# A decoder layer with routed experts on one core: expert results scattered to the tokens' rows, two routing phases run as one pipeline after the attention, and two heads per column group of the values product

## The chip, the cores and the metric

The kernel runs on one core of a Trainium2 chip. The metric is device microseconds of one execution; the median of three runs is given. A core has TensorE for matrix products (PE; its weight loads, PEld, overlap them), VectorE (DVE), ScalarE (ACT), GpSimd (POOL) and SyncE (SP), which here only issues transfers. Each engine works through its own instructions in order, and they meet through semaphores. Sixteen DMA engines move data for all of them.

## The reference

32 sequences of 128 tokens, width 128. All is float32.

```
x = layernorm(x + attention(x, x, x, causal))          # 16 heads of 8
x = layernorm(x + attention(x, ctx, ctx))              # cross attention
r = softmax(x @ router_w + router_b)                   # 8 experts
topw, topi = top_k(r, 2); topw = softmax(topw)
h_e = gelu(x @ w1[e] + b1[e])                          # 128 -> 512, exact gelu
o_e = h_e @ w2[e] + b2[e]                              # 512 -> 128
x = layernorm(x + sum over the token's two experts of topw * o_e)
```

The reference computes all experts for all tokens and weighs six of eight by zero. The kernel computes most tokens for their two experts only.

## The kernel before

**Attention.** A group is four sequences; there are eight groups of self attention ("s") and eight of cross attention ("c"). A unit is one sequence of one kind, 64 in all. `order` (L873) puts eleven self units first, then one cross and one self in turn, then the last eleven cross units. Time in the program is counted in half slots, two to a unit: `half_slot(h)` (L947) issues the scores of the newest unit and the transposed scores of the one two before it (`both_scores`, L355), each half of 16 heads; the maximum over keys (DVE, L390), the exponential (ACT, L398), and for self attention the causal mask (POOL, L402). In even half slots follow the values product of the unit three back (`values`, L429) and the turning of the newest maxima; in odd ones the splitting of maxima (POOL, L407) and `outputs` (L443), which transposes the result, divides by the sum and stores it. The values of a group lie in one of three tiles `vs` (L213), nine columns a head: eight values and a one, which makes the sum. A values product takes 32 such columns as its weights, so its result has 32 rows a head, of which nine are used; four heads stand above one another and four such sets fill a bank.

After that, `half_slot` runs whatever `table` holds for h: fetching inputs, transposing them, projections of keys, queries and values, `project` (output projection, residual and norm), `keep_x2`, `route` (top two experts and their weights, five steps), `place` (five steps) and `scatter`. Thus the order on every engine is written out by hand: `at(h, call)` fixes it.

**Routing.** Groups 0 to 3 are phase 0, groups 4 to 6 phase 1. `place` gives each of a token's two choices a row in `xs`, a DRAM buffer cut in blocks of 128 rows that belong to one expert each: eight first blocks, one an expert, and up to 31 or 23 more, whose expert stands in `ph.tab`. `scatter` (L634) sends tokens' rows there by indirect DMA on POOL, two of 128 rows in a half slot. `clear` has zeroed the rows that nobody fills.

**Blocks** (L675). For each block SP fetches its expert's packed weights (578 KB, `wd`, five buffers, four ahead); for four blocks at once it fetches rows (`xt`), PE transposes them and DVE copies them out (`turn`). `first_layer` is four products and four GELUs on ACT; `second_layer` of the block before is four products into one tile, to which DVE adds the bias (L755) into `ot`; after four blocks SP stores `ot` to `eo` in the same order of rows. Phase 0's 39 blocks run at half slot 117, between two stretches of attention (`BURST`); phase 1's 31 run after the last scatter.

**Sums.** `gather` (L780) brings a token's two result rows from `eo` by indirect DMA on POOL; `combine` (L791) adds them to the token's row by weight, on DVE, and `finish` norms and stores it. Phase 0's gathers lie in the half slots after the first blocks, phase 1's beside the dense group.

**Dense group** (L817). Group 7 isn't scattered. All eight experts are computed for its 512 tokens at the end, with a product of 512 columns, and each result is added by its weight, which is zero for most.

Constants and parameters are set up ahead of everything (L130 to L267), on all queues; nineteen parameter loads are issued from ACT's queue and the others from SP's. The main order, L966 on:

```
for h in range(-2, 2 * BURST + 3): half_slot(h)
bursts[0].run(lambda: None)
...          # half slots until the last scatter
bursts[1].prepare()
bursts[1].run(beside)
...          # dense group, with the gathers and sums of phase 1 beside it
```

Of the kernel before, what the change touches and what calls it, by code (L numbers as in the profile page):

```python
# [17 lines left out]
P = 128  # L18
# [6 lines left out]
PHASES = ((0, 4), (4, 3))  # L25
NP = len(PHASES)
LAST = 7
# [12 lines left out]
VS = HD + 1  # L40
NPART = 3
LEAD = 11
BURST = 57
# [15 lines left out]
def kernel(  # L59
# [69 lines left out]
    groups = {(kind, gi): Group(kind, gi) for kind in "sc" for gi in range(NG)}  # L129
    fetch(groups["s", 0])  # L130

    def load(src, shape, name, queue=nc.scalar):
        t = const.tile(shape, F32, name=name)
        queue.dma_start(out=t, in_=src)
        return t

    def column(src, name, queue=nc.scalar):
        return load(src.rearrange("(p o) -> p o", o=1), [P, 1], name, queue)
# [6 lines left out]
    class Attn:  # L145
        def __init__(self, wq, bq, wk, bk, wv, bv, wo, n):
            self.wk = load(wk, [P, P], f"wk{n}")
            self.bk = column(bk, f"bk{n}")
            self.wq = load(wq, [P, P], f"wq{n}")
            self.bq = column(bq, f"bq{n}")  # L150
            self.wv = load(wv, [P, P], f"wv{n}")
            self.wo = load(wo, [P, P], f"wo{n}")
            self.bv = column(bv, f"bv{n}")

    sa = Attn(sa_wq, sa_bq, sa_wk, sa_bk, sa_wv, sa_bv, sa_wo, "s")
# [4 lines left out]

    causal = const.tile([P, RG, P], BF16, name="causal")
    nc.gpsimd.memset(causal, 0.0)
    nc.gpsimd.affine_select(
        out=causal,
        in_=causal,
        pattern=[[0, RG], [-1, P]],
        compare_op=ALU.is_ge,
        fill=MASKED,
        base=0,
        channel_multiplier=1,  # L170
    )
# [22 lines left out]

    mp4 = setup.tile([P, RG, NPART, 4], F32, name="mp4")
# [9 lines left out]
    ones16 = const.tile([P, P], BF16, name="ones16")  # L205
    nc.gpsimd.memset(ones16, 1.0)
# [4 lines left out]


    vs = [const.tile([P, G, H * VS + VC - VS], F32, name=f"v_{i}") for i in range(3)]  # L213
    for t in vs:
        nc.gpsimd.memset(t, 0.0)
        nc.gpsimd.memset(
            t[:, :, : H * VS].rearrange("p b (h c) -> p b h c", c=VS)[:, :, :, HD:], 1.0
        )
    apart = const.tile([1, 1], F32, name="apart")
    mhalf = const.tile([P, G], F32, name="mhalf")  # L220
    nc.gpsimd.memset(mhalf, -0.5)

    def counted(shape, pattern, base, name, pool=const):
# [7 lines left out]
    bo_s = row(sa_bo, P, "bo_s")  # L231
    ca = Attn(ca_wq, ca_bq, ca_wk, ca_bk, ca_wv, ca_bv, ca_wo, "c")
    head_bias(ca, "c")
    bo_c = row(ca_bo, P, "bo_c")
    lng = [row(a, P, f"lng{i}") for i, a in enumerate((ln1_g, ln2_g, ln3_g))]
    lnb = [row(a, P, f"lnb{i}") for i, a in enumerate((ln1_b, ln2_b, ln3_b))]
    lngT = [column(a, f"lngT{i}") for i, a in enumerate((ln1_g, ln2_g))]
    lnbT = [column(a, f"lnbT{i}") for i, a in enumerate((ln1_b, ln2_b))]
    rw = load(router_w, [P, E], "rw")
    rb = row(router_b, E, "rb")  # L240
    b1 = setup.tile([E * NFC, P], F32, name="b1")
    nc.sync.dma_start(out=b1, in_=e_b1.rearrange("e (c f) -> (e c) f", f=P))


    iota_e = counted([P, E], [[1, E]], 0, "iota_e")
    before16 = const.tile([P, P], BF16, name="before16")
    nc.gpsimd.affine_select(
        out=before16, in_=ones16, pattern=[[1, P]], compare_op=ALU.is_gt,
        fill=0.0, base=0, channel_multiplier=-1,
    )  # L250
    full = counted([P, E, G], [[0, E], [P, G]], 0, "full")
    e_col = counted([P, E, E], [[1, E], [0, E]], 0, "e_col", setup)
    e_row = counted([P, E, E], [[0, E], [1, E]], 0, "e_row", setup)
    lower = const.tile([P, E, E], F32, name="lower")
    nc.vector.tensor_tensor(lower, e_row, e_col, ALU.is_lt)
    d_at = counted([P, max(ND), E], [[1, max(ND)], [0, E]], NS, "d_at")
    zero = const.tile([P, P], F32, name="zero")
    nc.gpsimd.memset(zero, 0.0)
# [5 lines left out]
    xs = [tc.dram_tile([NBL[p] * P, P], F32, name=f"xs_{p}") for p in range(NP)]  # L264
    eo = [tc.dram_tile([NBL[p] * P, P], F32, name=f"eo_{p}") for p in range(NP)]
# [69 lines left out]
    turn = {"v": 0, "m": 0}  # L335
# [93 lines left out]
    def values(u):  # L429
        po = mm_tile([P, RG, P], f"po_{u.name}")  # L430
        for g in range(RG):
            for r in range(4):
                h = 4 * g + r
                nc.tensor.matmul(  # L434
                    po[VC * r : VC * r + VC, g, :],
                    lhsT=u.group.v[:, u.b, VS * h : VS * h + VC],
                    rhs=u.pr[:, h, :], start=True, stop=True,
                )
        u.group.done += 1
        u.uT = prob.tile([P, RG, P], F32, tag="uT", name=f"uT_{u.name}")  # L440
        nc.scalar.copy(u.uT, po)

    def outputs(u):  # L443
        if u.b == 0:
            u.group.o = act.tile([P, G, P], F32, tag="o", name=f"o_{u.group.name}", bufs=3)
        pu = mm_tile([P, RG, 4, VC], f"pu_{u.name}")
        for g in range(RG):
            nc.tensor.transpose(pu[:, g].rearrange("p r c -> p (r c)"), u.uT[:, g, :], ident)
        pu = pu.rearrange("p g r c -> p (g r) c")
        ri = small.tile([P, H], F32, tag="ri", name=f"ri_{u.name}")  # L450
        nc.vector.reciprocal(ri, pu[:, :, HD])
        nc.vector.tensor_tensor(
            u.group.o[:, u.b, :].rearrange("p (h d) -> p h d", d=HD),
            pu[:, :, 0:HD],
            bc(ri, 2, HD),
# [32 lines left out]
    def keep_x2(gr):  # L488
        gr.x2T = affineT(gr, 1)
        gr.x2 = act.tile([P, G, P], F32, tag="x2", name=f"x2_{gr.gi}", bufs=3)  # L490
        nc.gpsimd.tensor_tensor(gr.x2, gr.y, bc(lng[1], 1, G), ALU.mult)
        nc.gpsimd.tensor_tensor(gr.x2, gr.x2, bc(lnb[1], 1, G), ALU.add)
        if gr.gi != LAST:
            nc.sync.dma_start(
                out=x2d[G * gr.gi : G * gr.gi + G].rearrange("b p d -> p b d"), in_=gr.x2
            )

    def route(gr):
# [31 lines left out]
        nc.vector.tensor_copy(idf, idx[:, :, 0:2])  # L530
        gr.onehot = small.tile([P, 2, G, E], F32, tag="onehot", name=f"onehot_{gi}", bufs=2)
        for k in range(2):
            nc.vector.tensor_tensor(
                gr.onehot[:, k], bc(iota_e, 1, G), bc(idf[:, :, k], 2, E), ALU.is_equal
# [9 lines left out]
    class Phase:  # L544
# [6 lines left out]
        def __init__(self, p):  # L551
            self.p, self.sent, self.first = p, [], True
# [3 lines left out]
    def place(gr, ph):  # L556
# [7 lines left out]
        if ph.first:  # L564
# [8 lines left out]
            nc.gpsimd.tensor_scalar(ph.at, iota_e, float(P), float(P), ALU.mult, ALU.add)  # L573
# [8 lines left out]
        nc.vector.tensor_tensor(over, bc(tot, 2, G), full, ALU.is_gt)  # L582
# [42 lines left out]
        nc.vector.tensor_tensor(which, bc(end, 1, ND[p]), d_at[:, : ND[p], :], ALU.is_le)  # L625
# [3 lines left out]
        if gi == PHASES[p][0] + PHASES[p][1] - 1:  # L629
            ph.tab = slot.tile([P, ND[p]], I32, tag=f"tab{p}", name=f"tab{p}")  # L630
            nc.vector.tensor_copy(ph.tab, ph.sums)
            nc.vector.tensor_scalar(ph.tab, ph.tab, E - 1, None, ALU.bitwise_and)

# [35 lines left out]
    def clear(p):  # L669
        nc.sync.dma_start(out=xs[p].rearrange("(n p) d -> p n d", p=P), in_=bc(zero, 1, NBL[p]))  # L670
# [4 lines left out]
    class Blocks:  # L675
# [3 lines left out]
        def __init__(self, ph):  # L679
            self.ph, self.n = ph, NBL[ph.p]  # L680
            self.xt, self.xT, self.ot, self.w, self.h = {}, {}, {}, {}, {}
# [7 lines left out]
        def fetch_rows(self, q):  # L689
# [3 lines left out]
            self.xt[q] = moe.tile([P, XB, P], F32, tag="xt", name=f"xt_{p}_{q}", bufs=1)  # L693
# [21 lines left out]
        def turn(self, q):  # L715
# [5 lines left out]
            for j in range(n):  # L721
                nc.tensor.transpose(px[:, j, :], xt[:, j, :], ident)
# [331 lines left out]
```

## Time and profile before

| | us |
|---|---|
| median of 3 runs (798.76 to 801.45) | 801.38 |
| the profiled execution | 799.84 |
| its span, first to last instruction | 798.1 |
| PE busy | 626.9 (79%) |
| PE weight loads busy | 505.7 (63%) |
| DVE busy | 419.4 (53%) |
| ACT busy | 370.7 (46%) |
| POOL busy | 326.4 (41%) |
| DMA moved | 84.46 MB, 106 GB/s over the span |

A profile page gives busy time, the same in 40 slices of the span, the DMA queues, the chain of work that ended last, and the costliest groups of instructions by line, each with its busy time, the mean of one in ns, and the idle time of its engine just before it with what ended that. Times of the prediction are of the one profiled execution, so its sum is made against 799.84.

### The profile page before, as it was taken

The page shows a single profiled execution, that of the slowest core. Times are in us where ns is not written, and L with a number is a line of the kernel's source. Part 1 is how long each engine was busy: PE and PEld are TensorE (multiplying, and loading weights), DVE is VectorE, ACT ScalarE, POOL GpSimd, SP SyncE. Part 2 cuts the span into 40 slices and gives each one's busy share as a digit, 9 for nine tenths or more (in the row PEclk, how much of TensorE's full clock was granted, in tenths as well). Part 3 has the DMA queues.
Part 4 walks back from the last instruction along what each step waited for, and adds up shares of the span by engine and source line. Part 5 has one row for each costly group of instructions (what it writes and reads, how often), then busy time and mean ns, then how long its engine had stood idle before and what let it go on. Part 6 is the DMA issues. An engine that isn't in the chain of part 4 may idle for free.

```text
span 798.1 us, 21600 instructions
## 1 busy us (share of the span) xinstructions
PE 626.9 (79%) x8943; PEld 505.7 (63%) x8995; DVE 419.4 (53%) x1242; ACT 370.7 (46%) x668; POOL 326.4 (41%) x616
## 2 busy tenths in 40 slices
PE   1889888889889889889988999985821299968882
PEld 0466667677667667667767899974721199835552
DVE  1344665657866767857867222275777222102574
ACT  0256565665655555645556655642300155523220
POOL 3135654425475474483572000058787300052320
PEclk9799999999999999999999999997855599979996
DMA  3060605301001001001023899712131689862121
GB/s 80 1 147 3 146 16 161 86 3 43 2 25 44 2 29 42 3 28 29 19 76 122 277 359 347 269 32 84 51 96 34 211 275 347 310 217 68 45 77 28
DMA packets 74115, 84.46 MB, mean 106 GB/s; under 512 B 7680, under 2 KB 61216, under 8 KB 74016
## 3 DMA queue, kind: packets, MB, share of 16 engines
q1 hardware_dynamic: 67696, 75.18, 29.6%
q0 software_dynamic: 3584, 7.35, 3.1%
q8 instruction: 71, 1.16, 0.6%
q10 hardware_dynamic: 2736, 0.53, 0.3%
q14 instruction: 28, 0.23, 0.1%
HBM read 66.25 MB, written 21.51 MB: 110 GB/s over the span
## 4 chain that ended last, share of the span: by engine, by line
PE 49%; POOL 16%; DVE 11%; DMA 11%; ACT 7%; issue 5%; SPq 1%; ACTq 0%; POOLq 0%; DVEq 0%
DMA wd<-wpk 8%; POOL xs L640 6%; PE st_s L375 5%; PE ph L733 5%; PE phd L848 4%; PE po L751 4%; PE pod L861 4%; PE po_s L434 3%; POOL gt L786 3%; PE st_c L375 2%; DVE m_s L390 2%; PE st_s L367 2%; PE sc_s L362 2%; DVE m_c L390 2%; PE po_c L434 2%
## 5 line engine op out<-in xcount | busy, mean ns | idle before, releaser
L390 DVE TENSOR_REDUCE m_s<-sc_s 128x8 f32<-128x1024 f32 x64 | 78.1, 1220 | 78.0 <-PE st_s L375 68.4
L738 ACT ACTIVATE h<-ph,wd 128x128 f32<-128x128 f32 x280 | 80.0, 369 | 72.6 <-PE ph L733 44.4
L402 POOL TENSOR_SCALAR_AFFINE_SELECT pr_s<-pr_s 128x1024 f32<-128x1024 f32 x64 | 70.0, 1094 | 105.2 <-ACT pr_s L398 105.0
L390 DVE TENSOR_REDUCE m_c<-sc_c 128x8 f32<-128x1024 f32 x64 | 78.0, 1219 | 48.4 <-PE st_c L375 37.7
L398 ACT ACTIVATE pr_s<-st_s 128x1024 f32<-128x1024 f32 x64 | 65.6, 1026 | 77.7 <-PE st_s L375 73.3
L398 ACT ACTIVATE pr_c<-st_c 128x1024 f32<-128x1024 f32 x64 | 65.6, 1026 | 73.5 <-PE st_c L375 69.0
L786 POOL DMA_INDIRECT gt<-eo,slots x56 | 55.4, 990 | 95.4 <-DMA eo<-ot 79.8
L382 PE MATMUL sc_c<-k_c,qb_c 32*128 32x128 f32 x1024 | 77.8, 292 | 8.8 <-DVE m_s L390 5.7
L733 PE MATMUL ph<-xT,wd 128*128 128x128 f32 x560 | 78.3, 285 | 7.0 <-DMA wd<-wpk 4.7
L755 DVE TENSOR_TENSOR ot<-po,wd 128x128 f32<-128x128 f32 x70 | 20.4, 291 | 115.6 <-PE po L751 115.6
L382 PE MATMUL sc_s<-k_s,qb_s 32*128 32x128 f32 x1024 | 77.8, 292 | 0.4 <-issue 0.4
L733 PEld LDWEIGHTS ph<-xT,wd 128*128 128x128 f32 x560 | 69.4, 195 | 12.3 <-DMA wd<-wpk 7.0
L751 PE MATMUL po<-wd,h 128*128 128x128 f32 x560 | 74.0, 276 | 1.3 <-ACT h L738 1.3
L375 PE MATMUL st_c<-qb_c,k_c 32*128 32x128 f32 x1024 | 74.8, 281 | 0.0
L375 PEld LDWEIGHTS st_c<-qb_c,k_c 32*128 32x128 f32 x1024 | 72.3, 194 | 0.5
L382 PEld LDWEIGHTS sc_c<-k_c,qb_c 32*128 32x128 f32 x1024 | 65.1, 193 | 11.7 <-DVE m_s L390 6.5
L375 PEld LDWEIGHTS st_s<-qb_s,k_s 32*128 32x128 f32 x1024 | 69.4, 192 | 0.0
L751 PEld LDWEIGHTS po<-wd,h 128*128 128x128 f32 x560 | 68.4, 193 | 1.5 <-ACT h L738 1.5
L375 PE MATMUL st_s<-qb_s,k_s 32*128 32x128 f32 x1024 | 69.0, 274 | 0.0
L382 PEld LDWEIGHTS sc_s<-k_s,qb_s 32*128 32x128 f32 x1024 | 65.3, 193 | 2.5 <-issue 2.1
L416 POOL CAST m<-m_c 128x16 bf16<-128x16 f32 x32 | 6.4, 199 | 139.7 <-DVE m_c L390 139.7
L640 POOL DMA_INDIRECT xs<-x,slots x56 | 57.2, 1022 | 11.0 <-issue 10.6
(221 smaller groups left out, 1235.1 us busy)
## 6 DMA issues: line engine op xcount, KB each, us to landing
wd<-wpk SPq DMA_DIRECT2D x70, 578.0 KB, 5.8
wd_d<-wpk SPq DMA_DIRECT2D x8, 578.0 KB, 4.5
wpk<-in_L_xattn_e_w_dram SPq DMA_DIRECT2D x16, 256.0 KB, 7.4
xt<-xs SPq DMA_DIRECT2D x16, 256.0 KB, 6.0
eo<-ot SPq DMA_DIRECT2D x16, 256.0 KB, 6.2
xs<-zero SPq DMA_DIRECT2D x1, 2496.0 KB, 11.8
xg<-in_x_dram SPq DMA_DIRECT2D x8, 256.0 KB, 3.4
eg<-in_ctx_dram SPq DMA_DIRECT2D x8, 256.0 KB, 3.3
```

What stands on the lines that cost most here:

```text
L375: nc.tensor.matmul(st[:, i, r, :], lhsT=old.group.k[rowsof(g), old.b, :], rhs=old.group.qb[rowsof(g), old.b, r, :], start=False, stop=r == 3,)
L382: nc.tensor.matmul(sc[:, i, r, :], lhsT=new.group.qb[rowsof(g), new.b, r, :], rhs=new.group.k[rowsof(g), new.b, :], start=not new.masked, ...
L390: nc.vector.tensor_reduce(new.m[:, 8 * half : 8 * half + 8], sc.rearrange("p i r k -> p (i r) k"), AX.X, ALU.max,)
L398: nc.scalar.activation(old.pr[:, hs, :], st.rearrange("p i r k -> p (i r) k"), AF.Exp, scale=SCALE)
L402: nc.gpsimd.affine_select(out=old.pr[:, hs, :], in_=old.pr[:, hs, :], pattern=[[0, 8], [1, P]], compare_op=ALU.is_ge, fill=0.0, base=0, ch ...
L434: nc.tensor.matmul(po[VC * r : VC * r + VC, g, :], lhsT=u.group.v[:, u.b, VS * h : VS * h + VC], rhs=u.pr[:, h, :], start=True, stop=True,)
L640: i = nc.gpsimd.indirect_dma_start(out=xs[ph.p][:, :], out_offset=bass.IndirectOffsetOnAxis(ap=slots[:, k, t : t + 1], axis=0), in_=gr.x2[ ...
L733: nc.tensor.matmul(hid[:, c, :], lhsT=w[:, c * P : (c + 1) * P], rhs=self.xT[i // XB][:, i % XB, :], start=True, stop=True,)
L738: nc.scalar.activation(self.h[i][:, c, :], hid[:, c, :], AF.Gelu, bias=w[:, B1 + c : B1 + c + 1])
L751: nc.tensor.matmul(po, lhsT=h[:, c, :], rhs=w[:, W2 + c * P : W2 + (c + 1) * P], start=c == 0, stop=c == NFC - 1,)
L786: nc.gpsimd.indirect_dma_start(out=gr.gt[:, k, b, :], out_offset=None, in_=eo[p][:, :], in_offset=bass.IndirectOffsetOnAxis(ap=slots[:, k, ...
L848: nc.tensor.matmul(hid[:, c % 2], lhsT=w[:, c * P : (c + 1) * P], rhs=self.gr.x2T, start=True, stop=True,)
```

## The change

Seven things change together.

1. *Phases.* Groups 0 to 5 are phase 0 (at most 55 blocks), 6 and 7 phase 1 (23). There is no dense group; group 7 is scattered like the others.
2. *One pipeline.* Both phases' blocks form one list, `Pipeline`, that starts at half slot 137, when all of phase 0 is scattered. The half slots that remain (137 to 152: routing, placing and scattering of groups 6 and 7) are issued one after each block. `prepare` stands at half slot 135.
3. *Results.* Each `second_layer` ends with an indirect DMA on POOL that scatters the 128 result rows to the rows of their tokens: in `eo` a token's two results now lie side by side behind an area for rows that nobody asked for. A row in `xs` carries two more columns for that, the token's row number and its first expert; `turn` works the destination out with four small DVE instructions. `ot` is one block, with four buffers.
4. *Sums.* `combine` fetches its results with one direct load on SP instead of eight gathers. Phase 0's six groups are summed beside the blocks of phase 1, two groups at a time, one step of each a block; phase 1's two groups after the last block.
5. *Values.* Two heads share a set of 32 rows: a head has 18 columns in `vs`, its own nine and nine zeros, and the second head's product is accumulated with its window moved by nine. `uT`, its transposes and its copy are half as large.
6. *Start.* An exponential on one element comes first on ACT. Only four loads (keys' and queries' weights and biases of self attention) stay on ACT's queue, the others go to SP's, several of them at later half slots (norms at 4, router at 5). Two of three fills of `vs` and the routing constants become steps of half slots 1, 7 and 9; the bias products (`pbv`) come after half slot 4.
7. `xt` has two buffers, and its next fetch is issued by the pipeline after `turn`, over the edge between the phases too.

```diff
-PHASES = ((0, 4), (4, 3))
+PHASES = ((0, 6), (6, 2))
...
-VS = HD + 1
+VW = HD + 1
+VS = 2 * VW
...
+TAG = P
+XW = P + 2
+FREE = [2 * P * n for n in NBL]
...
+    apart = const.tile([1, 1], F32, name="apart")
+    nc.gpsimd.memset(apart, 0.0)
+    nc.scalar.activation(apart, apart, AF.Exp)
     fetch(groups["s", 0])
...
-    def load(src, shape, name, queue=nc.scalar):
+    def load(src, shape, name, queue=nc.sync):
...
     def values(u):
-        po = mm_tile([P, RG, P], f"po_{u.name}")
...
+        po = mm_tile([P, 2, P], f"po_{u.name}")
+        for g in range(2):
+            for e in range(2):
+                for r in range(4):
+                    h = 2 * (4 * g + r) + e
+                    at_v = VS * h - VW * e
+                    nc.tensor.matmul(
+                        po[VC * r : VC * r + VC, g, :],
+                        lhsT=u.group.v[:, u.b, at_v : at_v + VC],
+                        rhs=u.pr[:, h, :], start=e == 0, stop=e == 1,
+                    )
...
+        nc.gpsimd.tensor_copy(gr.x2[:, :, TAG], rowno[:, G * gr.gi : G * gr.gi + G])
...
+        nc.vector.tensor_copy(gr.x2[:, :, TAG + 1], idf[:, :, 0])
...
+            nc.vector.tensor_tensor(
+                row[:, 0, :n], xt[:, :n, TAG + 1], self.ph.expert[:, XB * q : XB * q + n],
+                ALU.not_equal,
+            )
+            nc.vector.scalar_tensor_tensor(
+                row[:, 1, :n], xt[:, :n, TAG + 1], 0.0, later["free"][:, XB * q : XB * q + n],
+                ALU.is_lt, ALU.mult,
+            )
+            nc.vector.tensor_tensor(row[:, 0, :n], row[:, 0, :n], row[:, 1, :n], ALU.add)
+            nc.vector.tensor_tensor(self.to[q][:, :n], row[:, 0, :n], xt[:, :n, TAG], ALU.add)
...
-            nc.vector.tensor_tensor(self.ot[q][:, i % XB, :], po, w[:, B2:], ALU.add)
-            if i % XB == self.width(q) - 1:
-                nc.sync.dma_start(
-                    out=eo[p][self.rows(q), :].rearrange("(n p) d -> p n d", p=P),
-                    in_=self.ot.pop(q)[:, : self.width(q), :],
-                )
+            ot = moe.tile([P, P], F32, tag="ot", name=f"ot_{p}_{i}", bufs=4)
+            nc.vector.tensor_tensor(ot, po, w[:, B2:], ALU.add)
+            nc.gpsimd.memset(apart, 0.0)
+            s = nc.gpsimd.indirect_dma_start(
+                out=eo[p][:, :],
+                out_offset=bass.IndirectOffsetOnAxis(
+                    ap=self.to[q][:, i % XB : i % XB + 1], axis=0
+                ),
+                in_=ot, in_offset=None,
+            )
+            for j in self.ph.done:
+                tc.declare_no_dep(s.ins, j.ins, reason="rows of their own")
+            self.ph.done.append(s)
...
+            self.turn()
+            before = None
+            for j, (k, i) in enumerate(self.all):
+                self.weights(j + AHEAD)
+                k.first_layer(i)
+                if before:
+                    before[0].second_layer(before[1])
+                before = k, i
+                if i % XB == min(2, k.width(i // XB) - 1):
+                    self.turn()
+                beside(k.ph, i)
+            before[0].second_layer(before[1])
...
+        i = nc.sync.dma_start(
+            out=gt,
+            in_=eo[p][first : first + 2 * P * G, :].rearrange(
+                "(b p k) d -> p b (k d)", p=P, k=2
+            ),
+        )
+        for j in phases[p].done:
+            tc.add_manual_dep(i.ins, j.ins.name, SYNC, reason="results")
...
+    start = max(2 * (len(units) + 2), ready)
+    at(start - 2, blocks.prepare)
...
+        def beside(ph, i):
+            if table or left[0] < 2 * (len(units) + 3):
+                half_slot(left[0])
+                left[0] += 1
+            if ph.p and i == 2:
+                g0, n = PHASES[ph.p - 1]
+                sums.extend(combine(groups["c", gi]) for gi in range(g0, g0 + n))
+            step()
```

## What the change should do to the time

> **What bounds the kernel now.** I read the page's slices first, which show that the span is not of one piece, and then asked for busy times by stage. The columns are stage, length, busy us (and instructions) of PE, PEld, DVE, ACT and POOL, granted clock, DMA share, GB/s.
>
> ```profile
> core 0: us, PE busy (x) PEld busy (x) DVE busy (x) ACT busy (x) POOL busy (x), PEclk, DMA share, GB/s
> 0.00:24.00 24.00, 6.69 (x22) 3.75 (x22) 3.03 (x17) 4.91 (x7) 6.74 (x32) 1.00 0.30 67
> 24.00:434.00 410.00, 360.52 (x6574) 279.63 (x6625) 266.82 (x681) 231.68 (x308) 209.75 (x428) 0.96 0.18 49
> 434.00:518.50 84.50, 79.22 (x665) 75.72 (x665) 19.45 (x52) 49.56 (x163) 0.91 (x1) 1.00 0.88 302
> 518.50:575.70 57.20, 40.93 (x741) 34.99 (x742) 37.65 (x132) 21.37 (x27) 41.13 (x69) 0.85 0.18 51
> 575.70:635.30 59.60, 12.52 (x104) 10.10 (x103) 38.34 (x178) 5.76 (x11) 39.55 (x55) 0.55 0.34 106
> 635.30:703.00 67.70, 63.72 (x523) 61.28 (x523) 14.14 (x41) 35.46 (x124) 0.00 (x0) 0.97 0.85 291
> 703.00:787.00 84.00, 63.34 (x320) 40.20 (x320) 37.45 (x138) 21.99 (x32) 27.25 (x31) 0.93 0.31 97
> 787.00:798.10 11.10, 0.00 (x0) 0.00 (x0) 2.50 (x6) 0.00 (x0) 1.04 (x1) 0.50 0.08 24
> ```
>
> The stages are: start; attention to half slot 116; 39 blocks; the rest of attention with gathers; a tail of routing, gathers and scatters in which PE works a fifth of the time; 31 blocks; the dense group; the last norm. In the block stages PE (94%) and DMA (85 to 88%) are both near full: 84.5/39 and 67.7/31 give 2.17 us a block. In the tail nothing is full. The waits and the chain say what holds the thin stages:
>
> ```profile
> ACT L314 <- DMA lngT<-in_L_xattn_ln_g_dram: 15.9, 1, 15.9
> POOL gt L786 <- DMA eo<-ot: 79.8, 2, 78.7
> ```
>
> ACT does its first arithmetic at 15.9 us, after issuing nineteen loads on its own queue. The 79.8 us are idle POOL time, which cost nothing: no block stage has POOL work. This last fact matters, because the change puts POOL work there. The end of the tail, from the chain in order of time (start, us, what):
>
> ```profile
> 625.44 5.20 DMA xs<-x,slots
> ...
> 630.72 2.62 DMA xt<-xs
> ...
> 633.39 1.13 PE px L722 x4
> ...
> 634.55 0.70 DVE xT L724
> ...
> 635.29 3.79 PE ph L733 x16
> ```
>
> From the issue of the last scatter to the first block's matmul pass 9.85 us.
>
> **The change, part by part.** *Start.* Only four loads stay on ACT's queue (0.45 to 0.54 us each there), and the table is fetched before them; so the first copy can start when the input's transposes end, at 5.2 instead of 17.2 us. The keys' weights and bias still have to land: I take −11 us (−8 to −12). Against it: moved SP loads (ten norm loads; the six lng and lnb rows took 3.2 and 3.8 us to issue) ahead of the fetches and weight packing behind them in SP's queue, `lnb1c` on DVE that may wait for them, two blank fills of `vs` (0.65 us grow by 293/167 to 1.15, plus 0.2) and the routing constants (some 2 us of POOL, 1.5 of DVE) among the first masked units. POOL's 1.09 us mask is queued behind those fills, and the value matmuls wait for the mask: +3 (0 to 6).
>
> *Two heads per column group.* Value matmuls stay 16 a unit. Transposes fall from 4 to 2: PE takes 0.66 us for four, of which 0.27 is latency, so two save 0.26. But they stand in odd half slots, and those without table work take 2.67 us with 1.9 busy, and with `project` in them 2.67 too: the loop scores, maximum (1.22 us), scores is the bound. So there I cost the saving at nothing; if that cover were gone it would be 64 x 0.26 = −17. The copy on ACT falls from 0.587 by 256 elements, at the slope (687−369)/384 = 0.83 ns of the GELU rows: 0.21 us. It tells where ACT's queue is the bound, behind the four 0.78 us query activations, 16 times: −3. The row numbers and tags add one 0.2 us POOL op per group and 0.2 on DVE, larger `which` tables for six groups 0.35: +1.5. Half slot 117 then begins at 434 − 11 + 3 − 3 + 1.5 = 424.5.
>
> *Half slots 117 to 136.* Those to 130 took 57 us with 21 gathers between the scatters and a wait for `eo` on POOL. Cross attention alone runs 2.4 to 3.0 us a half slot elsewhere in this trace: 14 x 2.65, plus 5 for POOL's norm, 2.5 us of x2 and the scatters, is 42. Half slots 131 to 136 are four pairs of scatters at 2 x 1.3, and two of leftover units: 15. Sum 57, to 481.5.
>
> *Hand-over.* Before, scatter to matmul was 9.85 us. Now four weight loads are issued ahead of it, and group 5's last two scatters follow the first row fetch, on POOL perhaps behind it; SP's second fetch then waits for them with weight loads queued behind. I take 10 (6 to 18): 491.5. The stage of 57.2 and the tail of 59.6 us have become these 57 + 10; groups 6 and 7 go beside blocks.
>
> *Blocks.* They become 55 + 23 = 78, 8 more, while the dense group's 84 us vanish, and 56 gathers of 0.99 us on POOL turn into 8 direct loads on SP. First 55: 2.17 each, 119.4. Output leaves by one indirect DMA per block in place of a direct one per four: the same 64 KB. On POOL that is 0.09 + 1.02 us per 2.17, behind DVE's output addition, with 16 scatters of groups 6 and 7 (at most 3.4 us a block, four in a row) between. Group 7's route is two Exps among GELUs, up to four table loads of 1.28; PE's place and route matmuls wait for DVE. +8 (3 to 20): 127.4, to 619.
>
> No row shows an indirect DMA in a block stage. The nearest are the last four scatters, issued under four weight loads:
>
> ```profile
> L640 POOL DMA_INDIRECT xs<-x,slots x56: 954/982/1303, 225.4 to 625.4; - x56
> DMA to landing us min/median/max: 2.2/2.3/6.0
> ```
>
> They are the 6.0. With four `ot` buffers, a block can't be faster than (0.3 + 1.1 + 5)/4 = 1.6 us by this row: hidden, with 2.3 us to spare. One rule speaks against the change: the Trainium skill, SBUF — State Buffer, "SBUF: two separate sides" says that while VectorE runs a two-port operation GpSimd can't write the descriptors of its DMAs, and its next section gives 3100 ns for a DMA that takes 620 alone. By that factor of five an issue is 4.9 us, and POOL bounds every block: 78 x 4.9 = 382 us where I have 199, 902 in all. By the row, with DVE busy 64 to 66% of the two stages around these scatters and gathers, the longest issue of 112 is 1.30. I take the row.
>
> *Second phase beside the sums.* 23 blocks share the DMA engines with six groups' sums: 256 KB x2, 512 KB results, 256 KB out. A block's 706 KB now take 84.5 x 0.88/39 = 1.91 us of all engines, so by bytes a group takes 2.8 us; I take 3.1, since the trace's 512-byte packets took 27 ns and the weights' 4,624-byte ones 207, 19 against 22 GB/s an engine. 23 x 1.91 + 6 x 3.1 = 62.5 us, or 68 at a share of 0.92 (the page's best slices show 9 tenths). DVE: per group eight additions of 0.33, norm 2.4, two of 0.69: 6.4; two groups per seven blocks is 1.83 a block, with 0.29 output and 0.37 turning 2.5: below 2.96. DVE's additions wait in order for `gt`, and SP's loads for the last scatters and for the out transfer that frees `acc`, with weight loads behind both: +4. Together 72 (55 to 85), to 691.
>
> *End.* Last output 1.3, scatter 1.1 + 1.3, loads 4.5, two groups on DVE 12.8, out 2.3, rest 1.7: 25, where 11 were: 716. Around the span lie 799.84 − 798.1 = 1.7; the median of the runs is 1.5 above this execution: 719.
>
> **Rivals.** *Blocks stall on the tail's steps* (0.2): in the tail the 14 half slots from 131 to the last scatter (626.4) took 3.6 us each on latencies alone; if the 16 half slots beside blocks hold PE's queue at that pace, 16 x (3.6 − 2.17) = 23 in place of my 8, and with the high hand-over +8: 742. *The sums hide and starting gains are whole* (0.15): second phase at 2.3 a block, 53, early costs nil: 697. *Scatter bounds the blocks* (0.04), slower: the place is `ot`, freed only when its scatter lands. My 78 blocks take 199 us; with the 82 us to the time before, 281/78 = 3.6 us a block is the point from which it decides: landing 4 x 3.6 − 0.3 = 14.1 us after POOL gets it, over twice the worst seen, or an issue of 3.5 on POOL. At 4.0 it would end at 832. *It doesn't do what it says* (0.06): row fetch or results wait on all scatters in order, and each phase edge drains: two drains of 10 and, with lost prefetch, 2.5 us a block: 719 + 20 + 26 = 765.
>
> **The numbers.** The plain sum has 0.55. The range 692 to 750 takes in both nearer rivals and the bounds of hand-over, beside work and second phase, not all at their ends at once. About 0.5% (4 us) can be told from no change here; faster 0.95, same 0.01, slower 0.04.
>
> **What would show it.** First score maximum near 14 us rather than 25; half slots of 2.67 unchanged; blocks of the first phase at 2.2 with DMA share near 0.9; scatters of 1.0 us landing within 6; second phase near 3 us a block with DMA, not DVE, late; about 25 us after the last matmul. I am wrong if DVE `ot` waits for DMA, or if odd half slots shrink by 0.26.

## The result, and the profile after

| | before | changed |
|---|---|---|
| median of 4 runs, us | 801.41 (798.76 to 802.09) | 742.60 (739.42 to 747.11) |
| ratio, 95% interval | | 0.9276 (0.9222 to 0.933) |
| the profiled execution | 799.84 | 743.56 |
| its span | 798.1 | 741.5 |
| PE busy | 626.9 (79%) | 596.9 (80%) |
| POOL busy | 326.4 (41%) | 364.7 (49%) |

The kernel is faster by 58.8 us. The forecast was 719, so it is 23.6 us slower than forecast, inside the range of 692 to 750. Busy times by stage of the changed kernel, in the columns shown ahead of the change; the stages are attention to half slot 116, the rest of it to the first block, 55 blocks, 23 blocks, and the end:

```profile
core 0: us, PE busy (x) PEld busy (x) DVE busy (x) ACT busy (x) POOL busy (x), PEclk, DMA share, GB/s
13.20:440.00 426.80, 370.28 (x6504) 277.76 (x6504) 274.60 (x702) 220.73 (x306) 215.24 (x443) 0.93 0.20 43
440.00:506.20 66.20, 45.87 (x808) 37.95 (x808) 46.76 (x186) 25.88 (x37) 31.75 (x73) 0.84 0.21 69
506.20:635.50 129.30, 115.65 (x951) 111.02 (x952) 42.97 (x196) 68.95 (x227) 76.25 (x142) 0.96 0.91 310
635.50:713.00 77.50, 55.01 (x380) 53.14 (x381) 40.38 (x172) 25.09 (x88) 30.87 (x56) 0.83 0.84 268
713.00:741.50 28.50, 2.00 (x17) 1.81 (x15) 15.13 (x54) 1.14 (x4) 6.19 (x11) 0.62 0.34 99
```

The thin tail and the dense group of before are gone, and the two block stages still run with DMA near full. Two things are to be seen beside that: the clock of the first stage is 0.93, where 24 to 434 us had 0.96 before, and the stage of 23 blocks has a lower DMA share (0.84) than the one of 55 (0.91), so it isn't bound by bytes all the time.

The new operation, the scatter of results. First the view of `eo` (duration min/median/max in ns), then three of the waits (us in total, times, longest):

```profile
L812 POOL DMA_INDIRECT eo<-ot,to x78: 954/966/1304, 512.6 to 717.3; - x78
...
DMA to landing us min/median/max: 2.2/5.2/8.5
```

```profile
DVE acc L889 <- DMA gt<-eo: 34.4, 6, 9.1
...
PE ph L789 <- DMA wd<-wpk: 30.9, 22, 5.3
...
DVE ot L810 <- DMA eo<-ot,to: 8.0, 4, 2.4
```

An issue takes what the scatters of before took, not five times as much, with DVE busy for 33% of the 55 blocks and 52% of the 23. (Whether any of DVE's operations beside them is of the two-port kind that the prediction's rule speaks of, no run shows.) DVE waits for an `ot` to come free four times, 8.0 us in all. The long waits are others: the sums for their rows, and the blocks for their weights.

The sum against the trace, stage by stage. The 434 from which the prediction counts lies 1.95 us after the start of the maximum of half slot 116 (432.05) before; the same point is at 439.2 after.

| stage | predicted | trace | error |
|---|---|---|---|
| start to the end of half slot 116 | 424.5 | 439.2 | +14.7 |
| to the first block | 67 | 67.0 | 0.0 |
| 55 blocks | 127.4 | 129.3 | +1.9 |
| 23 blocks | 72 | 77.5 | +5.5 |
| end | 25 | 28.5 | +3.5 |

Maxima (DVE, L390 before, L425 after) stand in both kernels and date every half slot. Their difference, after less before: −12.1 us at half slot 0 (25.31 and 13.19), −11.2 at 8, −4.8 at 12, −4.9 at 28, −0.8 at 48, +2.1 at 64, +4.7 at 100, +5.2 at 116. The 15.9 us for which ACT waited for `lngT` are gone. So the start gained what was forecast, half slots 8 to 12, where the constants lie, took 6.4 of it back, and from half slot 12 to 116 the attention, which was to be 1.5 us shorter, lost another 10.0. Taken half slot by half slot, 8.9 of the 10.0 came in the 24 that meet a stretch of half clock in one of the two kernels or begin within 1.5 us after it, 2.6 between the maxima of half slots 32 and 36 (of which at the end), and −1.5, as forecast, in the other 76.

*Half slot 9.* From the timeline of the changed kernel (start, duration, engine, line; idle time before it and what ended it in brackets):

```profile
50.89 1.29 POOL L386 TENSOR_TENSOR xg<-xg,bo_s 128x512 f32<-128x512 f32 x1
...
52.56 0.17 DVE L238 CAST iota_e<-iota_e_i 128x8 f32<-128x8 int32 x1 [3.05 <-POOL iota_e_i L236]
...
55.91 1.22 DVE L425 TENSOR_REDUCE m_s<-sc_s 128x8 f32<-128x1024 f32 x1
57.18 1.01 PE L397 MATMUL sc_s<-causal,ident 128*128 128x512 bf16 x2 [4.68 <-DVE m_s L425]
```

The number fills on POOL stand behind the addition `xg`. DVE waits for the first of them with the casts in its queue, the maximum stands behind the casts, and the scores' tile that PE needs is freed by that maximum. PE is idle for 4.68 us, and the record of the clock then shows half speed from 54.6 to 61.4.

*The clock in the attention.* The same place in both kernels: half slots 56 to 58. Before, then after:

```profile
220.82 0.66 PE L448 MATMUL pu_c<-ident,uT_c 128*128 128x128 f32 x4
...
223.04 0.39 PE L367 MATMUL st_c<-mq_c,ones 32*128 32x512 bf16 x2 [1.56 <-ACT pr_s L398]
...
224.25 1.08 PE L434 MATMUL po_s<-pr_s,v 128*32 128x128 f32 x32
```

```profile
222.20 0.44 PE L486 MATMUL pu_c<-ident,uT_c 128*128 128x128 f32 x2
...
224.41 0.39 PE L402 MATMUL st_c<-mq_c,ones 32*128 32x512 bf16 x2 [1.77 <-ACT pr_s L433]
...
225.93 1.94 PE L472 MATMUL po_s<-pr_s,v 128*32 128x128 f32 x32
```

Both wait for the exponential, which stands behind four query activations on ACT. With two transposes fewer, PE waits 1.77 us instead of 1.56, as the argument that the saving is worth nothing would have it. But then the same 32 value products take 1.94 us instead of 1.08. The windows say why (before; after):

```profile
219.40:222.80 3.40, 1.93 (x39) 1.60 (x39) 2.61 (x6) 3.40 (x5) 0.06 (x1) 1.00 0.02 5
```

```profile
221.80:225.20 3.40, 1.63 (x46) 1.36 (x41) 1.91 (x5) 2.56 (x4) 0.77 (x1) 1.00 0.00 0
225.20:228.60 3.40, 3.40 (x55) 2.69 (x48) 1.65 (x2) 1.40 (x2) 2.76 (x9) 0.50 0.04 13
```

PE was busy for 1.63 of 3.40 us instead of 1.93, and the next 3.4 us were granted at half clock. From the maximum of half slot 57 to that of 59 before needs 7.15 us, after 8.69. Between 60 and 430 us the clock record has 5 such stretches before (17.0 us at half clock) and 11 after (44.2 us).

### The profile page after: what moved, and what is told of

Read it like the earlier page. It is cut to its first block, busy times and chain, and to the rows that moved or that the text cites. A ratio compares the mean times of both kernels' runs of the same rounds, so it can differ in the third digit from the quotient of the medians.

```text
span 741.5 us, 21324 instructions
## 1 busy us (share of the span) xinstructions
PE 596.9 (80%) x8691; PEld 486.4 (66%) x8691; DVE 421.4 (57%) x1313; ACT 347.8 (47%) x671; POOL 364.7 (49%) x744
## 4 chain that ended last, share of the span: by engine, by line
PE 43%; DVE 17%; POOL 13%; DMA 13%; issue 6%; ACT 6%; SPq 1%; DVEq 0%; POOLq 0%
DMA wd<-wpk 7%; POOL xs L684 6%; PE st_s L410 5%; PE ph L789 5%; DVE m_c L425 5%; PE sc_s L397 4%; PE po L805 4%; PE po_s L472 4%; PE st_c L410 3%; DMA eo<-ot,to 3%; PE po_c L472 3%; ACT qb_s L365 3%; DVE m_s L425 2%; PE sc_s L417 2%; PE st_s L402 2%
## 5 line engine op out<-in xcount | busy, mean ns | idle before, releaser
L794 ACT ACTIVATE h<-ph,wd 128x128 f32<-128x128 f32 x312 | 88.8, 368 | 120.6 <-PE ph L789 84.1
L789 PE MATMUL ph<-xT,wd 128*128 128x128 f32 x624 | 94.2, 298 | 39.6 <-DMA wd<-wpk 30.9
L812 POOL DMA_INDIRECT eo<-ot,to x78 | 77.1, 988 | 99.0 <-DVE ot L810 36.4
L425 DVE TENSOR_REDUCE m_s<-sc_s 128x8 f32<-128x1024 f32 x64 | 78.1, 1221 | 83.8 <-PE st_s L410 67.5
L789 PEld LDWEIGHTS ph<-xT,wd 128*128 128x128 f32 x624 | 83.2, 207 | 46.2 <-DMA wd<-wpk 33.4
L433 ACT ACTIVATE pr_s<-st_s 128x1024 f32<-128x1024 f32 x64 | 65.6, 1025 | 94.0 <-PE st_s L410 88.1
L425 DVE TENSOR_REDUCE m_c<-sc_c 128x8 f32<-128x1024 f32 x64 | 78.0, 1220 | 54.3 <-PE st_c L410 40.9
L805 PE MATMUL po<-wd,h 128*128 128x128 f32 x624 | 89.1, 290 | 1.9 <-ACT h L794 1.9
L805 PEld LDWEIGHTS po<-wd,h 128*128 128x128 f32 x624 | 82.8, 206 | 2.1 <-ACT h L794 2.1
L417 PE MATMUL sc_s<-k_s,qb_s 32*128 32x128 f32 x1024 | 82.4, 303 | 0.2 <-ACT qb_s L365 0.2
L410 PEld LDWEIGHTS st_s<-qb_s,k_s 32*128 32x128 f32 x1024 | 73.1, 200 | 1.1 <-issue 1.1
L410 PE MATMUL st_s<-qb_s,k_s 32*128 32x128 f32 x1024 | 72.8, 283 | 0.9 <-issue 0.9
L684 POOL DMA_INDIRECT xs<-x,slots x64 | 63.8, 997 | 15.7 <-issue 12.0
L397 PE MATMUL sc_s<-causal,ident 128*128 128x512 bf16 x128 | 41.1, 405 | 24.7 <-DVE m_s L425 13.7
```

Source lines behind the costliest of these rows:

```text
L397: nc.tensor.matmul(sc[:, i], lhsT=ident16, rhs=causal, start=True, stop=False)
L410: nc.tensor.matmul(st[:, i, r, :], lhsT=old.group.k[rowsof(g), old.b, :], rhs=old.group.qb[rowsof(g), old.b, r, :], start=False, stop=r == 3,)
L417: nc.tensor.matmul(sc[:, i, r, :], lhsT=new.group.qb[rowsof(g), new.b, r, :], rhs=new.group.k[rowsof(g), new.b, :], start=not new.masked, ...
L425: nc.vector.tensor_reduce(new.m[:, 8 * half : 8 * half + 8], sc.rearrange("p i r k -> p (i r) k"), AX.X, ALU.max,)
L433: nc.scalar.activation(old.pr[:, hs, :], st.rearrange("p i r k -> p (i r) k"), AF.Exp, scale=SCALE)
L684: i = nc.gpsimd.indirect_dma_start(out=xs[ph.p][:, :], out_offset=bass.IndirectOffsetOnAxis(ap=slots[:, k, t : t + 1], axis=0), in_=gr.x2[ ...
```

## The experiments

The theory: the 15 us of the first stage are the constants' chain and the half-clock stretches that PE's new idle time brings, and the second phase is late because the sums' loads wait in SP's queue ahead of weights. Rivals: the stretches are chance or belong to the new start; the two heads' other work (windows, copies) costs the time; POOL's scatters hold the blocks; the sums cost what their bytes cost.

The twelve runs were made in three sets, each on one chip. On the first two chips the kernel before took 817.34 and 818.62 us, on the third 802.98. Ratios are to the kernel before on the same chip, and kernels are compared with one another within a set only. The changed kernel itself wasn't run in the first two, so there the variants have only one another and the kernel before beside them, and the times that the expectations name, which are those of the first result's chip, can't be met as they stand.

**First set.** *Two heads alone*: the kernel before with the new values.

```diff
-VS = HD + 1
+VW = HD + 1
+VS = 2 * VW
...
-                    lhsT=u.group.v[:, u.b, VS * h : VS * h + VC],
-                    rhs=u.pr[:, h, :], start=True, stop=True,
+                        lhsT=u.group.v[:, u.b, at_v : at_v + VC],
+                        rhs=u.pr[:, h, :], start=e == 0, stop=e == 1,
...
-        for g in range(RG):
+        for g in range(2):
```

> The kernel before with the two heads per column group alone. Clock theory (less TensorE work in odd half slots means more windows with TensorE under some 60% busy, and each of them halves the granted clock for 3.4 us, at about 1.4 us lost): the attention to half slot 116 grows by 5 to 10 us and the half-clock stretches between 60 and 430 us rise from 5 to about 11, so 806 to 811 us. Rival (the shifted window, its accumulation or the wider value tile costs time itself): also 806 to 811, but with the number of half-clock stretches as before. As the prediction had it (ACT's shorter copy, nothing else): 798.

*One head*: the inverse, on the changed kernel (`VS = VW` and the old `values` and `outputs`).

> The changed kernel with one head per column group, as before. Clock theory: the maximum of half slot 116 comes 6 to 10 us earlier than the 437.3 of the changed kernel, with about 5 half-clock stretches in the attention in place of 11, and the total is 733 to 737. Rival (the drift comes from the row numbers and tags of the x2 tile, or from later transfers): no change, 743; as the prediction had it, 3 us slower, 746.

*Four transposes*: the changed kernel, with each of its two transposes made twice and the second results unread.

```diff
-        pu = mm_tile([P, 2, 4, VC], f"pu_{u.name}")
-        for g in range(2):
-            nc.tensor.transpose(pu[:, g].rearrange("p r c -> p (r c)"), u.uT[:, g, :], ident)
+        pu = mm_tile([P, RG, 4, VC], f"pu_{u.name}")
+        for g in range(RG):
+            nc.tensor.transpose(pu[:, g].rearrange("p r c -> p (r c)"), u.uT[:, g % 2, :], ident)
```

> The changed kernel, two heads kept, but with four transposes a unit in place of two: the two extra ones repeat the same input and nobody reads them. Clock theory: more TensorE work makes it faster, 733 to 737, with 4 to 7 half-clock stretches in the attention. Rival (accumulation or the value tile costs the time): no gain, 743 or more.

*Constants early*: number fills on POOL in the setup, the casts on DVE spread over four half slots.

```diff
-    at(9, routing_constants)
+    at(11, cast, "iota_e", "full")
+    at(13, lower_of)
+    at(15, cast, "d_at", "free")
+    at(17, row_numbers)
```

> The changed kernel with the routing constants' POOL instructions at the start, while POOL is idle, and their DVE casts spread over half slots 11, 13, 15 and 17. If the step of half slot 9 (DVE's maximum behind casts that wait for POOL, TensorE idle 4.7 us, then half a clock for 6.8 us) is what took away 6 of the 12 us won at the start: 736 to 738. Rival (units after half slot 9 wait for something else that was hidden behind it, such as the loads in SP's queue): 741 to 743.

| | median us | ratio (95%) | half-clock stretches, 60 to 430 us | maximum of half slot 116 |
|---|---|---|---|---|
| two heads alone | 821.68 | 1.0045 (1.002 to 1.0071) | 12 (40.8 us) | 454.6 |
| one head | 772.71 | 0.9433 (0.9411 to 0.9455) | 6 (30.6 us) | 449.0 |
| four transposes | 772.42 | 0.9435 (0.9405 to 0.9465) | 5 (20.4 us) | 442.6 |
| constants early | 768.52 | 0.94 (0.9363 to 0.9436) | 10 (34.0 us) | 438.9 |

The two heads alone make the kernel before slower, by 1.6 to 5.8 us, where the prediction had −3 and the clock theory 5 to 10. Over 60 to 430 us of the profiled execution its granted clock is 0.94, that of the kernel before 0.98 (an execution on another chip):

```profile
60.00:430.00 370.00, 328.25 (x6125) 257.26 (x6174) 249.18 (x656) 217.15 (x288) 197.06 (x396) 0.98 0.16 46
```

```profile
60.00:430.00 370.00, 321.77 (x5719) 241.66 (x5718) 233.36 (x601) 193.75 (x270) 187.13 (x375) 0.94 0.14 38
```

Nor is it one execution's chance: over all runs of this set, each of the ten of the two heads has a mean clock of 0.897 to 0.907, and each of the fifteen of before has 0.909 to 0.921. So the lower clock comes with this part, whatever the start is. (At least two of the twelve stretches follow waits that only these chips have, of which at the end.) One head and four transposes can't be told apart in time: nothing else of the two heads shows. From half slot 12 to 116, leaving out 32 to 36, they take 360.1 and 360.4 us; *constants early*, with its two transposes, takes 366.4. Over all runs the clocks of four transposes (0.894 to 0.915) and of constants early (0.891 to 0.905) overlap. The constants work at their place: half slot 16 is at 73.1 us, and at 86.5 with one head and 80.3 with four transposes, on the same chip.

**Second set.** *Filler*: four transposes, and eight more of the identity, unread, after each group's queries.

```diff
+    def warm(n):
+        pw = mm_tile([P, G, P], "warm")
+        for b in range(n):
+            nc.tensor.transpose(pw[:, b % G, :], ident, ident)
...
+            at(2 * t0 - 3, warm, 8)
```

> The changed kernel with four transposes a unit as in the run before, and eight more transposes of the identity, read by nobody, at the end of the half slot after each queries step, where TensorE waits 1.8 us for ACT's query activations. Clock theory: 0 to 3 half-clock stretches in the attention, and 729 to 734. Rival (the stretches have another cause, or the filler delays the scores behind it): not below the four transposes alone.

*Direct store*: a block's result goes out with one direct store on SP; the placing of results is left out.

```diff
-            nc.gpsimd.memset(apart, 0.0)
-            s = nc.gpsimd.indirect_dma_start(
...
+            r = FREE[p] + P * i % (2 * P * G * PHASES[p][1])
+            s = nc.sync.dma_start(out=eo[p][r : r + P, :], in_=ot)
```

> The changed kernel with one direct store per block on SP in place of the indirect scatter on POOL; the results then lie in the order of blocks, so the sums add wrong rows: the placing of results is left out. Prediction's step (scatter hidden behind the blocks): the blocks keep their pace within 3 us in all, 740 to 746. Rival (issue or landing of the scatter is what the blocks wait for): 10 us or more faster.

*Sums after*: all eight groups are summed after the last block.

```diff
-            if ph.p and i == 2:
-                g0, n = PHASES[ph.p - 1]
-                sums.extend(combine(groups["c", gi]) for gi in range(g0, g0 + n))
-            step()
+            pass
...
-        sums.extend(combine(groups["c", gi]) for gi in range(g0, g0 + n))
+        sums.extend(combine(groups["c", gi]) for gi in range(NG))
```

> The changed kernel with all eight groups' sums after the last block. If the 77 us of the second phase's 23 blocks are those of the sums' loads and their waits: the 23 blocks take 44 to 50 us and the end 28 + 6 x 6.4 = 66 us, 748 in all, about 5 slower. Rival (the second phase is slow of itself, by its edge and its weights): its blocks stay at 70 or more, 775.

*Loads ahead*: the loads of `combine` become a step of their own, `sum_loads`, with four buffers; a pair's additions start four or five blocks after its loads.

```diff
+            if ph.p and i in (3, 7, 12):
+                k = (3, 7, 12).index(i)
+                for gi in (2 * k, 2 * k + 1):
+                    sum_loads(groups["c", gi])
+            if ph.p and i in (7, 12, 17):
+                k = (7, 12, 17).index(i)
+                sums.extend(combine(groups["c", gi]) for gi in (2 * k, 2 * k + 1))
```

> The changed kernel with each pair of sums' loads issued four to five blocks ahead of its additions, with four buffers in place of two. If DVE's 34 us of waiting for these loads, with the blocks' outputs behind them in its queue, are what makes the second phase slow: 728 to 734. Rival (the DMA engines are full in any case): 740 to 743.

| | median us | ratio (95%) | blocks 17 to 34 | 23 blocks | end |
|---|---|---|---|---|---|
| filler | 769.62 | 0.9382 (0.9351 to 0.9412) | 41.7 | 76.1 | 30.2 |
| direct store | 769.06 | 0.9389 (0.9342 to 0.9435) | 36.9 | 76.3 | 29.0 |
| sums after | 799.06 | 0.9722 (0.9674 to 0.9769) | 43.1 | 46.0 | 77.5 |
| loads ahead | 767.30 | 0.9359 (0.933 to 0.9388) | 44.7 | 65.6 | 31.1 |

Without scatters the blocks from 17 to 34 are 4.8 to 7.8 us shorter than in the others; the next twenty take 41.6, no less than 40.5 to 41.7. So the scatters are hidden in a plain block and cost some 6 us where group 7's places and scatters share POOL and DVE with them. Over the whole kernel this set can't tell direct stores, filler and loads ahead from one another: the intervals overlap. The filler's half-clock stretches are 5 (17.0 us), where 0 to 3 were expected; from half slot 12 to 116 without 32 to 36 it takes 364.7 us, the other three 366.5 to 369.4. Summing after the blocks gives the 23 blocks alone: 46.0 us, 2.0 a block, at a DMA share of 0.98.

```profile
673.60:719.60 46.00, 44.76 (x381) 43.28 (x382) 11.62 (x47) 25.09 (x88) 22.79 (x45) 1.00 0.98 340
```

With the sums beside them they take 76; so 30 us of the second phase are due to the sums. Yet beside the blocks is the better place: after them the end takes 77.5 us, 48 more, and the kernel is some 30 us slower than the others of its set, where 5 were expected. A third of the 30 goes when the loads are issued earlier, with four buffers instead of two; no run separates the two. The timeline of the changed kernel at the second phase's edge shows what is queued (SPq is the queue on SP):

```profile
646.01 2.25 SPq L876 DMA_DIRECT2D gt<-eo  x1
648.36 1.13 SPq L750 DMA_DIRECT2D wd<-wpk  x1
...
652.25 1.14 DVE L889 SCALAR_TENSOR_TENSOR acc<-gt,wts,acc 128x128 f32<-128x128 f32 x4 [6.80 <-DMA gt<-eo]
...
656.22 1.08 POOL L812 DMA_INDIRECT eo<-ot,to  x1 [9.43 <-DVE acc L889]
```

The weights' load stands behind the loads for the sums, the addition has nothing to add for 6.80 us, and the block's result, on DVE behind the addition, reaches POOL after 9.43.

**Third set.** The changed kernel itself; then constants early and loads ahead together; then four transposes on top; then the filler on top of that.

> The changed kernel itself, on the chip of the next three, to compare them with. The runs of variants came out at ratios of 0.936 to 0.944 to the kernel before, on chips where that took 817 to 819 us. If their differences are small, the changed kernel is at 0.943 to 0.945 there, about 772 us. If instead the variants all lost something, it is at 0.928 again, 759.

> The changed kernel with the routing constants early and the sums' loads ahead, two transposes a unit. If the two gains are independent (6 and 6 to 10 us): 12 to 15 us under the changed kernel in this call. If the clock's half stretches take back what is won early: 6 to 9.

> The kernel of the run before with four transposes a unit, two of which nobody reads. Clock theory: half-clock stretches in the attention fall from about 10 to 5, each worth 1.4 us: 5 to 8 us faster than the run before. Rival (the stretches are a sign and cost nothing, since another engine holds the half slots in which they fall): within 2 us of it.

> The kernel of the run before with eight more transposes of the identity behind each queries step. Clock theory: stretches fall to 5 or below, and the time by a further 1 to 5 us; rival: the filler stands in front of the scores and costs its own time, 0 to 6 us slower.

| | median us (runs) | ratio (95%) | half slot 12 | half slot 116 | half-clock stretches, 60 to 430 us | 23 blocks | end |
|---|---|---|---|---|---|---|---|
| changed kernel | 745.63 (742.25 to 751.26) | 0.9291 (0.9251 to 0.9331) | 66.9 | 443.9 | 13 (47.6 us) | 79.2 | 28.5 |
| constants, loads | 726.11 (722.8 to 731.05) | 0.9054 (0.9012 to 0.9095) | 60.0 | 437.0 | 13 (47.6 us) | 63.5 | 31.1 |
| + four transposes | 723.22 (717.69 to 725.31) | 0.9016 (0.8971 to 0.9061) | 58.6 | 428.4 | 5 (23.8 us) | 63.5 | 31.1 |
| + filler | 719.09 (717.5 to 725.14) | 0.8993 (0.8945 to 0.904) | 59.8 | 426.7 | 4 (13.6 us) | 63.4 | 31.2 |

The changed kernel is back at its first ratio and the variants run here are all faster than it, so the higher ratios of the first two sets belong to their chips. From half slot 12 to 116 these take 377.0, 377.0, 369.9 and 366.9 us: the constants and the loads do nothing there, and two more transposes a unit, work that nobody reads, save 7.1. The profiled executions of the first two kernels were the slowest of their runs; the changed kernel's first profile has 373.4. Without half slots 32 to 36 it is 359.1, 359.3, 350.1 and 349.0, in the changed kernel's first profile 356.8, and 349.4 before. So two executions of one kernel differ by 2.3 there, and the transposes gave 6.7 to 9.2. The two half slots shown above, 57 and 58, took 8.71, 8.75, 7.14 and 7.15 us. The window from 60 to 430 us for the second, third and fourth:

```profile
60.00:430.00 370.00, 327.42 (x5851) 248.47 (x5845) 244.38 (x640) 200.49 (x280) 190.69 (x387) 0.94 0.19 41
```

```profile
60.00:430.00 370.00, 332.47 (x6058) 255.58 (x6057) 249.93 (x667) 203.59 (x283) 193.43 (x395) 0.97 0.19 41
```

```profile
60.00:430.00 370.00, 341.86 (x6197) 265.33 (x6185) 252.83 (x672) 205.37 (x286) 195.32 (x395) 0.98 0.19 41
```

PE is busier, DVE, ACT and POOL get more done in the same 370 us, and the clock is 0.94, 0.97, 0.98. In the medians the step to four transposes is 2.9 us, where 5 to 8 were expected, and the next 4.1; single steps are within the intervals. Of the clock there is no doubt: over all their runs it is 0.911 to 0.921, 0.926 to 0.940 and 0.936 to 0.942. The profiles show the step larger than the medians do, since that of the second kernel was its slowest run. The last kernel is the fastest measured, 26.5 us below the changed one on its chip.

The 23 blocks of the first two kernels, without and with the loads ahead:

```profile
641.50:720.70 79.20, 55.66 (x381) 53.34 (x382) 40.05 (x171) 25.07 (x88) 30.65 (x55) 0.81 0.82 258
```

```profile
634.80:698.20 63.40, 49.35 (x381) 47.82 (x382) 38.99 (x167) 25.17 (x88) 29.00 (x51) 0.92 0.96 322
```

PE and ACT do the same work in 15.8 us less, at a DMA share of 0.96. The end is 2.6 us longer, so 13 remain.

## Why the forecast was right in kind and 24 us short

- *Start, −11.* Right: −12.1.
- *"+3 (0 to 6)" for the early costs.* Mis-sized: +7.4 by half slot 12. The sum took 2 us of POOL and 1.5 of DVE as durations. It didn't say what was queued behind the waiting engine: the casts wait for POOL, the maximum stands behind the casts, PE behind the maximum. 4.68 us of PE and then 6.8 at half clock followed. Moving the fills and spreading the casts took 6.9 off half slot 12 (66.9 to 60.0).
- *"So there I cost the saving at nothing", and −3 for the copies.* This is the step that failed. The saving of PE's time was indeed worth nothing as time, and the copies did shrink. But nothing was not the worst that could come of it: with less to do, TensorE was granted a lower clock (0.897 to 0.907 against 0.909 to 0.921 over all runs of two heads alone and before). From half slot 12 to 116 the trace has +10.0 where the sum had −1.5, and 8.9 of it in half slots at half clock. Two heads alone gave a ratio of 1.0045, and four transposes took back 6.7 to 9.2 in the third set and 6.0 in the first. I had named "odd half slots shrink by 0.26" as the way to be wrong, and looked at one side only.
- *Half slots 117 to 136 and hand-over, 67.* 67.0, by luck: in the hand-over, scatter to first block took 12.35 us instead of my 10, and the half slots took 54.7 instead of 57. The chain of waits has the reason that was named as a risk:

```profile
493.86 2.66 DMA xs<-x,slots
...
496.81 2.78 DMA xt<-xs
...
501.75 0.96 POOL xs L684
```

The last scatters stand on POOL until the first rows are fetched; POOL's next fill (L613) stands behind them, DVE waits 5.65 us for that, and the copies that turn the rows follow on DVE.
- *55 blocks, 127.4.* 129.3. At the 2.17 a block from which I counted it is +9.9 for my +8: 7.1 in the first sixteen, beside half slots, 4.0 in 17 to 34, into which group 7's last scatters fall, and −1.2 in the last 21. The rival *blocks stall on the tail's steps* gave 742, which is the time measured, but not its cause: it asked for +23 here.
- *Scatters hidden.* Right but for some 6 us, in blocks 17 to 34. *Scatter bounds the blocks* was to show in DVE waiting for DMA. That sign did come, with 8.0 us in four waits, three of them between 543 and 567 us, in blocks 15 to 25; as a bound it didn't.
- *Second phase, 72.* 77.5. The bytes were right: with loads ahead it takes 63.4 to 63.5 at a share of 0.96, and the sum by bytes was 62.5. The term for waits in SP's and DVE's queues, "+4", was the one that was too small: it is 79.2 − 63.5, about 16 in the third set, 14 by the changed kernel's first profile (77.5), and 10.5 in the second set. I had taken 68 for the bytes and 4 for the waits; the one was 4.5 too high and the other 10 to 12 too low.
- *End, 25.* 28.5, of the same kind: loads, then DVE.

The repairs together gave 26.5 us where the sum was 25.5 short (741.5 against 716). That the two agree is in part chance: nothing was repaired in the 55 blocks or the end.

What stays open. The four half slots from the maximum of 32 to that of 36 are 2.6 to 5.8 us longer than before's in all four kernels of the third set and in the changed kernel, while the DMA engines are full with the clearing of `xs`. It writes 5,070 KB where 4,480 were cleared before, 1.13 times the bytes, in rows of 520 bytes instead of 512; but from 110 to 152 us the packets of the queue that does it take 79% of the 16 engines' time, where they took 43% before. PE waits there for nothing that the profile shows; no run moved the clearing or kept its rows at 512 bytes.

On the chips of the first two sets all kernels were slower: before by 2%, and the changed ones more. Their traces show ACT and DVE held, often together, for 2 to 6 us in waits that the profile puts down to `remote`, that is to no instruction of this core, and that the other chips' traces don't have; those looked at lie in half slots and blocks that have an indirect DMA on POOL; the first sixteen blocks took 50 to 53 us there and 41 to 42 on the other chips. With direct stores it was 49.7. The instructions' durations are the same (the maximum 1.22 us, the exponential 1.02, a scatter 0.99 in the mean). The cause isn't known.

## What to carry to other kernels

When a change takes work from TensorE in a stage where it waits for others, look at how full it stays in a few microseconds, not only that the work is off the path: here windows of 3.41 us with TensorE busy for less than 0.64 often lost the clock, and 32 products in the stretch after took 1.94 us instead of 1.08. When a step puts a wait on an engine, price what is queued behind the wait: constants of 3.5 us cost 7, and sums that fit by bytes cost 10 to 16 until their loads were issued some blocks ahead. And a forecast that agrees with the time for a rival's reason has still to be checked stage by stage.

## What the runs showed of the hardware

The clock. In the attention of the changed kernel no gap of PE between 60 and 430 us is longer than 2.2 us, and yet the clock was halved eleven times. The Trainium skill, TensorE: Matmul & The Clock Gate, "Why this matters for your kernels", asks for no idle gaps over some 3 us; the measurement is stricter. Windows of 3.41 us at full clock on the record's own grid, with PE busy below half, were always followed by half clock in the changed kernel and before; with half to 0.64 they went either way, 6 of 8 to half clock in the changed kernel and 2 of 7 before; above that always to full clock. In other runs windows of 0.69, 0.73 and 0.83 lost it and one of 0.48 kept it; so the busy share as the profile models it isn't exactly what the clock goes by, and what is stays open. The same page's note on a second mode, where frequent short idling makes the clock swing, is nearer to what is seen here.

DMA. From 591 to 635 us, in the last 21 of the 55 blocks, the engines moved 354 GB/s at a share of 1.01; a block of 706 KB then needs 2.04 us.

```profile
591.10:635.50 44.40, 41.17 (x361) 40.27 (x361) 12.69 (x52) 24.55 (x87) 23.17 (x44) 1.00 1.01 354
```

The Trainium skill, DMA: Bandwidth & Descriptors, "Specifications", gives about 358 GB/s as a core's limit of memory, and the mean of the row is near it. But single slices of 1.1 us in this stretch reach 421, so it isn't shown that this is what bounds these blocks; the engines themselves were busy all the time. The scatters landed 2.2 to 8.5 us after they were issued, most of the time beside weights, and four buffers were enough.
